# Moving some products of two state space loops from VectorE to GpSimd

## The chip, the cores and the metric

The kernel runs on one core of a Trainium2 chip, as one program for a whole network of four layers. A core has five engines with a queue of instructions each: TensorE (PE in the profile, with its weight loads as PEld), VectorE (DVE), ScalarE (ACT), GpSimd (POOL) and SyncE (SP), which here issues the DMAs. Each engine works its queue in order and waits on semaphores for the others.

The metric is the device time of one execution in microseconds. Before the change the median of 3 runs was 2389.74 us (2386.41 to 2395.51).

## The reference

The network is a chain of residual blocks on x of shape (4, 512, 128). Two of the blocks, `L2_attn_b` and `L3_attn_b`, are selective state space layers of the same form. Cut to what matters, one of them is

```python
xz = x @ in_proj                                # 256 inner channels and 256 gates
u = silu(causal_conv4(xi) + conv_b)             # xi, z = the halves of xz
dtr, Bc, Cc = split(u @ x_proj)                 # 64, 16 and 16 columns
delta = softplus(dtr @ dt_proj + dt_bias)
A = -exp(A_log)                                 # 256 channels x 16 states
def step(h, inp):
    d_t, b_t, c_t, u_t = inp
    dA = exp(d_t[:, :, None] * A)               # the decay
    h = dA * h + (d_t * u_t)[:, :, None] * b_t[:, None, :]
    return h, einsum('bdn,bn->bd', h, c_t)
y = scan(step) over 512 tokens
out = ((y + u * D) * silu(z)) @ out_proj
```

Four batches, 256 channels, 16 states and 512 tokens make 4 x 256 x 16 = 16384 independent recurrences of 512 steps in each of the two layers.

## The kernel before

The function `mamba` runs once for `L2b` and once for `L3b`. A *unit* n is 256 recurrences: two halves t, each of 8 channels by 16 states on the 128 partitions, with 512 tokens along the free dimension, so a unit's tiles are 128 x 2 x 512. There are 16 units per batch and 64 units per loop, n = 0 to 63. One unit passes these steps:

- `fetch(n)` (L2424): two DMAs on SP bring delta of the unit's channels, repeated over the states, from DRAM into a ring of six SBUF buffers `da`.
- `decay(n)` (L2439): two ScalarE activations, exp(A * delta), in place in `da`. The first column of the second half holds 0, set once, which restarts the recurrence there; the activation and the DMA leave it out.
- `gain(n)` (matmuls through the helper at L346): TensorE spreads delta*u from the channels over the 128 rows, into a PSUM tile `ps_du` of two banks, three buffers.
- `product(n)` (L2453): VectorE multiplies `ps_du` by B, in place in PSUM.
- `scan(n)` (L2458): VectorE's scan computes h = a*h + x over 1024 columns, a from `da`, x from `ps_du`, the result into an SBUF tile `hc` with seven buffers. Then GpSimd multiplies `hc` by C in place (L2463); VectorE does this for the last unit alone (L2461).
- `read(n)`: for a pair of units, eight matmuls sum over the states into `ps_y`.

The main loop (L2515) sets the order by hand. In iteration n it traces fetch(n+5), product(n+1), scan(n), gain(n+2), decay(n+3), then the *pieces* whose time has come, and in odd iterations read(n-5) for units n-5 and n-4. Compute instructions are pinned behind what was traced before them on their engine (`keep`, `pin=True`), so this is also the order in each of the four queues.

The pieces prepare the next batch beside the current one (`prepare`, L2280): the convolution in four parts (c0a, c0b, c1a, c1b) with a ScalarE activation `raw` after each second part; u (Silu); xd, a projection copied to SBUF by ScalarE (L2325); dt0 and dt1, each a matmul and two activations that read its bank, `dl` and `e` (L2291); br and cr (projections of B and C); exps and logs (softplus); z0, z1 and sz (the gate); and s00 to s13, eight sums on GpSimd (L2356) with two stores of delta to DRAM (L2360). Counted from the first unit of the batch prepared, the usual times are

```python
order = (
    "c0a", "c0b", "c1a", "c1b", "u", "xd", "dt0", "dt1", "br", "exps", "logs", "s00",
    "s01", "z0", "s02", "s10", "z1", "s11", "cr", "s12", "s03", "sz", "s13",
)
usual = (
    -6, -5, -4, -3, -2, -1, 0, 1, 2, 3, 4, 5,
    6, 6, 7, 8, 8, 9, 9, 10, 11, 11, 12,
)
```

Batches 2 and 3 use these; so dt0 of batch 2 is in iteration 16 and that of batch 3 in iteration 32. Batch 1 is prepared from iteration 0 on by its own list. While batch 3 runs, nothing is left to prepare.

PSUM has eight banks: six for `ps_du`, one for `ps_y`, and a single one, tag "mm", that all the matmuls of the pieces share. When consecutive ScalarE functions are in different tables, a table load (ACT_TABLE_LOAD) stands before the second: Silu or Ln in the pieces, Exp in the decays. Copies in the trace are not preceded by one.

Of the kernel before, what the change touches and what calls it, by code (L numbers as in the profile page):

```python
# [11 lines left out]
F32 = mybir.dt.float32  # L12
AF = mybir.ActivationFunctionType
ALU = mybir.AluOpType
# [4 lines left out]
P = 128  # L19
B, S, D = 4, 512, 128  # L20
# [254 lines left out]
class Net:  # L275
# [1977 lines left out]
    def mamba(self, g):  # L2253
# [5 lines left out]
        nc, tc = self.nc, self.tc  # L2259
        LAG, SPREAD, AHEAD, FETCH = 4, 2, 3, 5  # L2260
        with ExitStack() as es:
            sp = es.enter_context(tc.tile_pool(name=g + "_s", bufs=1))
            rp = es.enter_context(tc.tile_pool(name=g + "_r", bufs=2))
            pp = es.enter_context(tc.tile_pool(name=g + "_p", bufs=1, space=PSUM))
            dp = es.enter_context(tc.tile_pool(name=g + "_d", bufs=2, space=DRAM))
            keep = tc.keep_in_program_order
            m0 = self.m
            w, am, wc, dram = m0["w"], m0["am"], m0["wc"], m0["dram"]
# [6 lines left out]
            def bank(name):  # L2275
                return pp.tile([P, S], F32, tag="mm", name=name)
# [3 lines left out]
            def prepare(b, **when):  # L2280

                u, sz, dl, du, br, cr = sets[b % 2]
                xb = b * S
                t = {}
# [29 lines left out]
                def project(out, at, n):  # L2314
                    ps = bank("ps_d")
                    for c in range(2):
                        self.mm(
                            ps[:n],
                            w["xp"][:, c * 320 + at : c * 320 + at + n],
                            u[:, c],  # L2320
                            start=c == 0,
                            stop=c == 1,
                            pin=True,
                        )
                    keep(nc.scalar.copy(out, ps[:n]))  # L2325

                def xd():
                    t["xd"] = rp.tile([64, S], F32, name="xd", bufs=1)
                    project(t["xd"], 0, 64)

                def step(c):
# [30 lines left out]
                for name, n in when.items():  # L2362
                    f = {
                        "c0a": (conv, 0, False),
                        "c0b": (conv, 0, True),
                        "c1a": (conv, 1, False),
                        "c1b": (conv, 1, True),
                        "u": (lambda: act(u, t["raw"], AF.Silu),),
                        "xd": (xd,),
                        "dt0": (step, 0),  # L2370
                        "dt1": (step, 1),
                        "br": (project, br, 64, P),
                        "cr": (project, cr, 192, P),
                        "exps": (exps,),
                        "logs": (logs,),
                        "z0": (gate, 0),
                        "z1": (gate, 1),
                        "sz": (lambda: act(sz, t["z"], AF.Silu),),
                        **{f"s{c}{k}": (sums, c, k) for c in range(2) for k in range(4)},
                    }[name]  # L2380
                    pieces.append((n, f))
# [10 lines left out]
            for b in range(2, B):  # L2392
                at = {p: 16 * (b - 1) + n for p, n in zip(order, usual)}
# [13 lines left out]
            dx, hc, yp, y, po = {}, {}, {}, {}, {}  # L2407
# [3 lines left out]
            da = {n: ring[n % 6] for n in range(16 * B)}  # L2411

            def place(n):
                b, k = divmod(n, 16)
                c, k = divmod(k, 8)
                i, h = divmod(k, 2)
                return b, c, i, h

            def fetch(n):

                b, c, i, h = place(n)
                for t in range(2):
                    m = 4 * (2 * t + h) + i
                    nc.sync.dma_start(  # L2424
                        da[n][:, t, t:],
                        dram[b][8 * m : 8 * m + 8, c, t:].unsqueeze(0).to_broadcast([16, 8, S - t]),
                    )

            def decay(n):
                b, c, i, h = place(n)  # L2430
                for t in range(2):
                    at = 16 * c + 4 * (2 * t + h) + i
                    src = da[n][:, t]
                    if n < SPREAD:
                        r = slice(64 * t, 64 * t + 64)
                        src = pp.tile([P, S], F32, tag="y", name="ps_dl") if t else bank("ps_dl")
                        self.mm(src, spread[r, 4 * h + i], sets[0][2][r, c], pin=True)
                    keep(
                        nc.scalar.activation(  # L2439
                            da[n][:, t, t:], src[:, t:], AF.Exp, scale=am[:, at : at + 1]  # L2440
                        )
                    )

            def gain(n):
                b, c, i, h = place(n)
                dx[n] = pp.tile([P, 2, S], F32, tag="du", name="ps_du", bufs=3)
                for t in range(2):
                    r = slice(64 * t, 64 * t + 64)
                    self.mm(dx[n][:, t], spread[r, 4 * h + i], sets[b % 2][3][r, c], pin=True)

            def product(n):
                br = sets[n // 16 % 2][4].unsqueeze(1).to_broadcast([P, 2, S])
                keep(nc.vector.tensor_tensor(dx[n], dx[n], br, ALU.mult))  # L2453

            def scan(n):
                hc[n] = rp.tile([P, 2, S], F32, name="hc", bufs=7)
                h, a, x = (t.rearrange("p t s -> p (t s)") for t in (hc[n], da[n], dx[n]))
                keep(nc.vector.tensor_tensor_scan(h, a, x, 0.0, ALU.mult, ALU.add))  # L2458
                cr = sets[n // 16 % 2][5].unsqueeze(1).to_broadcast([P, 2, S])
                if n == 16 * B - 1:  # L2460
                    keep(nc.vector.tensor_tensor(hc[n], hc[n], cr, ALU.mult))  # L2461
                else:
                    keep(nc.gpsimd.tensor_tensor(hc[n], hc[n], cr, ALU.mult))  # L2463

            def read(n):

                b, c, i, _ = place(n)
                if n % 8 == 0:
                    yp[c] = pp.tile([P, S], F32, tag="y", name="ps_y")
                    self.mm(yp[c], skip[:, c], sets[b % 2][0][:, c], stop=False, pin=True)  # L2470
                    if c == 0:
                        y[b] = rp.tile([P, 2, S], F32, name="y", bufs=1)
                for h in range(2):
                    for t in range(2):
                        r = 32 * (2 * t + h)
                        self.mm(
                            yp[c][r : r + 32],
                            gather[:, i],
                            hc[n + h][:, t],
                            start=False,  # L2480
                            stop=i == 3,
                            pin=True,
                        )
# [18 lines left out]
            if g == "L2b":  # L2502
                self.roots(B - 1, B, keep)
            self.prime(AF.Exp)
            decay(0)
            gain(0)
            gain(1)
            product(0)
            if g == "L2b":
                self.centred(B - 1, keep)  # L2510
            decay(1)
            for n in range(SPREAD, FETCH):
                fetch(n)
            decay(2)
            for n in range(16 * B + 10):  # L2515
                if n + FETCH < 16 * B:
                    fetch(n + FETCH)
                if n + 1 < 16 * B:
                    product(n + 1)
                if n < 16 * B:  # L2520
                    scan(n)
                if n + 2 < 16 * B:
                    gain(n + 2)
                if n + AHEAD < 16 * B:
                    decay(n + AHEAD)
                while pieces and pieces[0][0] < n + 1:
                    f, *a = pieces.pop(0)[1]
                    f(*a)
                m = n - 1 - LAG
                if n % 2 == 1 and 0 <= m < 16 * B:  # L2530
                    read(m)
                    if m % 8 == 6:
                        last = m == 16 * B - 2
                        plan.at(n if last else n + 1, gated, m // 16, m // 8 % 2)
                        if m % 16 == 14:
                            plan.at(n if last else n + 4, output, m // 16)
                            plan.at(
                                n if last else n + 5,
                                lambda b: self.add_to_x(b, po[b], keep),
                                m // 16,  # L2540
                            )
                plan.run(n)
# [472 lines left out]
```

## Time and profile before

| | |
|---|---|
| median of 3 runs | 2389.74 us |
| profiled execution: its own time | 2384.57 us |
| profiled execution: span | 2382.5 us |
| mean granted TensorE clock | 0.944 |
| PE busy | 2131.7 us (89%) |
| VectorE busy | 1700.4 us (71%) |
| ScalarE busy | 1267.4 us (53%) |
| GpSimd busy | 630.7 us (26%) |
| first loop, unit 0's scan to unit 63's | 1570.79 to 1798.2 us |
| second loop, unit 0's scan to unit 63's | 2103.00 to 2335.8 us |

The two loops are about a fifth of the span. The shares above are over the whole program; what bounds the loops is read from windows inside them.

How to read the profile's lines. A group line gives the line of the code, the engine, the operation, out<-in by the program's names, the shapes and the count; then busy us in all and the mean ns of one; then the idle time of that engine just before these instructions and what ended most of it ("<-PE ps_du L346": a matmul that wrote ps_du). A window line gives the stretch, its length, then the busy us of PE, PEld, DVE, ACT and POOL with counts, then the granted clock, the share of the DMA engines and GB/s. A timeline line gives start, duration, engine, line, operation and count, with the idle time before it in brackets.

### The profile page before, as it was taken

To read this page: it belongs to the slowest core of one execution; us is meant where nothing else is said; L and a number is where in the kernel's file an instruction comes from. 1 tells how busy PE (TensorE), PEld (TensorE's weight loads), DVE (VectorE), ACT (ScalarE), POOL (GpSimd) and SP (SyncE) were. 2 spreads that over 40 slices of the span, in tenths; PEclk is the share of its full clock that TensorE was granted. 3 is DMA by queue.
4 is the path that set the end of the run, shared out by engine and by line. 5 is a ranking of instruction groups with operands and counts; after the bars stand their busy time and mean duration, and the time that the engine had idled before them with its cause. 6 is when DMAs were issued, how large, how long until landed. Compare 5 with 4: busy or idle time off the path is not lost. (4 is left out here: it accounts for less than half of the span.)

```text
span 2382.5 us, 33560 instructions
## 1 busy us (share of the span) xinstructions
PE 2131.7 (89%) x12196; PEld 1012.4 (42%) x12196; DVE 1700.4 (71%) x3219; ACT 1267.4 (53%) x2531; POOL 630.7 (26%) x474
## 2 busy tenths in 40 slices
PE   7999999999899998999877789988869998878868
PEld 2343334643233334568545446542214666422213
DVE  6666666579999774756455664678997657688995
ACT  4555554159855665343343453666644445476643
POOL 1001000010000001021354510048872015148871
PEclk9999999999799998999879989999989999998989
DMA  3000000600000000600200015344552520044550
GB/s 146 1 1 1 1 1 15 130 1 2 1 2 3 1 1 1 133 11 2 109 1 1 0 39 96 71 124 146 156 149 46 113 38 2 1 133 141 155 154 18
DMA packets 68884, 127.84 MB, mean 54 GB/s; under 512 B 9328, under 2 KB 29296, under 8 KB 68080
## 3 DMA queue, kind: packets, MB, share of 16 engines
q1 hardware_dynamic: 68720, 125.71, 20.4%
q8 instruction: 96, 1.57, 0.3%
q14 instruction: 68, 0.56, 0.1%
HBM read 119.91 MB, written 5.64 MB: 53 GB/s over the span
## 5 line engine op out<-in xcount | busy, mean ns | idle before, releaser
L2463 POOL TENSOR_TENSOR hc<-hc,cr 128x1024 f32<-128x1024 f32 x126 | 297.5, 2362 | 113.6 <-DVE hc L2458 107.9
L2458 DVE TENSOR_TENSOR_SCAN hc<-da,ps_du 128x1024 f32<-128x1024 f32 x128 | 291.0, 2275 | 0.0
L346 PE MATMUL ps_s<-k,q 32*128 32x512 f32 (+3 forms) x1088 | 247.8, 597 | 13.4 <-DVE mx L853 4.8
L540 ACT ACTIVATE e<-ps_s,mx 128x512 f32<-128x512 f32 x256 | 172.6, 686 | 139.4 <-DVE mx L535 132.8
L346 PE MATMUL ps_du<-du,spread 64*128 64x512 f32 x512 | 161.7, 704 | 64.2 <-DVE hc L2458 63.9
L2439 ACT ACTIVATE da<-da,am 128x512 f32<-128x512 f32 x248 | 165.7, 715 | 62.1 <-DMA da<-dram 48.4
L346 PE MATMUL ps<-xT,w_L2f 128*128 128x512 f32 (+1 forms) x416 | 190.6, 605 | 0.2 <-DVE t L2030 0.2
L939 DVE TENSOR_REDUCE nm<-ps_s 128x1 f32<-128x512 f32 x256 | 162.4, 683 | 36.6 <-PE ps_s L346 26.4
L1025 ACT ACTIVATE e<-ps_st 128x512 f32<-128x512 f32 x256 | 138.3, 595 | 89.2 <-PE ps_s L346 61.5
L535 DVE TENSOR_REDUCE mx<-ps_s 128x2 f32<-128x1024 f32 x128 | 150.9, 1219 | 43.8 <-PE ps_s L346 43.6
L2453 DVE TENSOR_TENSOR ps_du<-ps_du,br 128x1024 f32<-128x1024 f32 x128 | 154.9, 1211 | 26.5 <-PE ps_du L346 26.4
L864 ACT ACTIVATE e<-e,mx 128x512 f32<-128x512 f32 (+3 forms) x256 | 140.1, 548 | 17.2 <-DVE mx L853 16.9
L346 PE MATMUL ps_st<-q,k 32*128 32x512 f32 x512 | 143.8, 646 | 0.0
L346 PE MATMUL ps_s<-q,k 64*128 64x512 f32 x512 | 129.1, 618 | 2.2 <-ACT e L540 1.7
L346 PE MATMUL ps_c<-e,vz 128*64 128x512 f32 x512 | 123.5, 604 | 0.8 <-POOL vz L551 0.8
L661 DVE TENSOR_TENSOR hc<-hc,wt 128x1024 f32<-128x1024 f32 x80 | 93.6, 1170 | 37.8 <-DMA wt<-dram 19.5
L2030 DVE SCALAR_TENSOR_TENSOR t<-ps,w_L2f,t 128x512 f32<-128x512 f32 (+1 forms) x104 | 76.9, 746 | 60.9 <-PE ps L346 37.3
L551 POOL TENSOR_TENSOR vz<-v,z 128x512 f32<-128x512 f32 x32 | 33.4, 1043 | 321.9 <-DVE z L549 292.9
L346 PEld LDWEIGHTS ps_du<-du,spread 64*128 64x128 f32 x512 | 45.4, 201 | 171.7 <-issue 126.4
L853 DVE CUSTOM_DVE_ANT_0 e<-ps_s,tri 128x512 f32<-128x512 f32 (+3 forms) x256 | 109.2, 484 | 12.3 <-PE ps_s L346 12.1
L346 PEld LDWEIGHTS ps_s<-k,q 32*128 32x128 f32 x1088 | 85.8, 192 | 75.5 <-issue 35.0
L346 PEld LDWEIGHTS ps<-xT,w_L2f 128*128 128x128 f32 (+1 forms) x416 | 74.7, 188 | 96.5 <-issue 79.0
(505 smaller groups left out, 4149.9 us busy)
## 6 DMA issues: line engine op xcount, KB each, us to landing
da<-dram SPq DMA_DIRECT2D x124, 256.0 KB
da<-dram SPq DMA_DIRECT2D x124, 255.5 KB
wt<-dram SPq DMA_DIRECT2D x144, 128.0 KB
wt<-dram SPq DMA_DIRECT2D x32, 256.0 KB
dram<-dl SPq DMA_DIRECT2D x16, 256.0 KB
wt<-dram SPq DMA_DIRECT2D x16, 224.0 KB
wt<-dram SPq DMA_DIRECT2D x16, 192.0 KB
wt<-dram SPq DMA_DIRECT2D x16, 160.0 KB
```

The costliest lines, as they stand in the source:

```text
L346: i = self.nc.tensor.matmul(out, lhsT, rhs, start=start, stop=stop)
L535: nc.vector.tensor_reduce(mx, sc, AX.X, ALU.max, negate=True)
L540: nc.scalar.activation(es[n][:, hh], sc[:, hh], AF.Exp, bias=mx[:, hh : hh + 1], accum_out=z[m][:, j, hh : hh + 1],)
L661: nc.vector.tensor_tensor(h, h, wt[b, k][:, r:e], ALU.mult)
L853: red = nc.vector.tensor_tensor_reduce(e[:, i, :w], sc[i][:, :w], tri[:, S - w :], -1.0, BIG, ALU.add, ALU.min, mx[:, i : i + 1],)
L864: nc.scalar.activation(e[:, i, :w], e[:, i, :w], AF.Exp, bias=mx[:, i : i + 1], scale=-1.0, accum_out=z[:, i : i + 1],)
L939: nc.vector.tensor_reduce(nm[:, j, i, 9:10], sc, AX.X, ALU.max, negate=True)
L1025: keep(nc.scalar.activation(es_[n][:, i], sc, AF.Exp))
L2439: nc.scalar.activation(da[n][:, t, t:], src[:, t:], AF.Exp, scale=am[:, at : at + 1])
L2453: keep(nc.vector.tensor_tensor(dx[n], dx[n], br, ALU.mult))
L2458: keep(nc.vector.tensor_tensor_scan(h, a, x, 0.0, ALU.mult, ALU.add))
L2463: keep(nc.gpsimd.tensor_tensor(hc[n], hc[n], cr, ALU.mult))
```

## The change

In each loop 11 of the 64 units, called *shared*, take another way: n = 2, 5, 15, 18, 31, 34, 47, 50, 53, 56 and 59. For a shared unit

- `product(n)` becomes a ScalarE copy of `ps_du` (128 x 1024) into the unit's `hc` tile and a GpSimd multiplication by B in place in `hc`;
- `decay(n)` writes its exponentials into the PSUM banks of `ps_du`, which the copy has read, and a third, small ScalarE copy brings the zero column along;
- `scan(n)` takes a from PSUM and x from `hc`, and writes `hc` in place.

In the order, gain and product of a shared unit n+2 are traced in iteration n before scan(n), and its decay after scan(n), in place of one iteration earlier. The decays of the other units stay three ahead. `hc` has eight buffers instead of seven, and the small tile xd lies in the `du` tile of the batch being prepared, which is written later.

```diff
                 def xd():
-                    t["xd"] = rp.tile([64, S], F32, name="xd", bufs=1)
+                    t["xd"] = du[:64, 0]
                     project(t["xd"], 0, 64)
...
                         self.mm(src, spread[r, 4 * h + i], sets[0][2][r, c], pin=True)
+                    out = dx[n] if n in shared else da[n]
                     keep(
                         nc.scalar.activation(
-                            da[n][:, t, t:], src[:, t:], AF.Exp, scale=am[:, at : at + 1]
+                            out[:, t, t:], src[:, t:], AF.Exp, scale=am[:, at : at + 1]
                         )
                     )
+                if n in shared:
+                    keep(nc.scalar.copy(dx[n][:, 1, 0:1], da[n][:, 1, 0:1]))
...
+            shared = (2, 5, 15, 18, 31, 34, 47, 50, 53, 56, 59)
+
             def product(n):
                 br = sets[n // 16 % 2][4].unsqueeze(1).to_broadcast([P, 2, S])
-                keep(nc.vector.tensor_tensor(dx[n], dx[n], br, ALU.mult))
+                if n in shared:
+                    hc[n] = rp.tile([P, 2, S], F32, name="hc", bufs=8)
+                    keep(nc.scalar.copy(hc[n], dx[n]))
+                    keep(nc.gpsimd.tensor_tensor(hc[n], hc[n], br, ALU.mult))
+                else:
+                    keep(nc.vector.tensor_tensor(dx[n], dx[n], br, ALU.mult))
 
             def scan(n):
-                hc[n] = rp.tile([P, 2, S], F32, name="hc", bufs=7)
-                h, a, x = (t.rearrange("p t s -> p (t s)") for t in (hc[n], da[n], dx[n]))
+                if n in shared:
+                    a, x = dx[n], hc[n]
+                else:
+                    hc[n] = rp.tile([P, 2, S], F32, name="hc", bufs=8)
+                    a, x = da[n], dx[n]
+                h, a, x = (t.rearrange("p t s -> p (t s)") for t in (hc[n], a, x))
                 keep(nc.vector.tensor_tensor_scan(h, a, x, 0.0, ALU.mult, ALU.add))
...
             for n in range(SPREAD, FETCH):
                 fetch(n)
-            decay(2)
             for n in range(16 * B + 10):
                 if n + FETCH < 16 * B:
                     fetch(n + FETCH)
-                if n + 1 < 16 * B:
+                if n + 1 < 16 * B and n + 1 not in shared:
                     product(n + 1)
+                if n + 2 in shared:
+                    gain(n + 2)
+                    product(n + 2)
                 if n < 16 * B:
                     scan(n)
-                if n + 2 < 16 * B:
+                if n + 2 in shared:
+                    decay(n + 2)
+                elif n + 2 < 16 * B:
                     gain(n + 2)
-                if n + AHEAD < 16 * B:
+                if n + AHEAD < 16 * B and n + AHEAD not in shared:
                     decay(n + AHEAD)
```

## The prediction

> **What bounds the kernel now.** I read the page's busy shares and slices first, then its costliest groups, then the table of windows over the two state space loops, last the timeline inside them. VectorE is called DVE, ScalarE ACT, GpSimd POOL and TensorE PE. These are the loop's groups (busy us, mean ns | idle before, releaser):
>
> ```profile
> L2463 POOL TENSOR_TENSOR hc<-hc,cr 128x1024 f32<-128x1024 f32 x126 | 297.5, 2362 | 113.6 <-DVE hc L2458 107.9
> L2458 DVE TENSOR_TENSOR_SCAN hc<-da,ps_du 128x1024 f32<-128x1024 f32 x128 | 291.0, 2275 | 0.0
> L2439 ACT ACTIVATE da<-da,am 128x512 f32<-128x512 f32 x248 | 165.7, 715 | 62.1 <-DMA da<-dram 48.4
> L2453 DVE TENSOR_TENSOR ps_du<-ps_du,br 128x1024 f32<-128x1024 f32 x128 | 154.9, 1211 | 26.5 <-PE ps_du L346 26.4
> ```
>
> The scans never idle, POOL mostly waits for them. The windows (busy us of PE, PEld, DVE, ACT, POOL) of the first loop say the same:
>
> ```profile
> 1620.00:1680.00 60.00, 53.09 (x194) 16.07 (x192) 59.04 (x47) 39.48 (x56) 50.73 (x27) 0.94 0.53 157
> 1680.00:1740.00 60.00, 50.02 (x186) 14.23 (x186) 59.41 (x46) 42.98 (x58) 50.34 (x27) 0.89 0.54 155
> 1740.00:1800.00 60.00, 39.25 (x164) 10.16 (x160) 59.83 (x45) 20.99 (x30) 40.70 (x18) 0.86 0.40 114
> ```
>
> DVE is busy 98 to 99.7% there. Scan starts on the timeline stand 3.31 us apart: 2.19 for the scan, 1.12 for the product between two scans (the last two scans, with no product between, take 4.45 us together). So a product is worth 1.12 us, less than its 1.21 us row, since neighbours overlap. By busy time PE has little to spare; ACT and POOL have most in the last window, where no next batch is prepared.
>
> The share does not say who waits for ACT. The timeline around units 16 to 20 does (rows of POOL, DMA and weight loads left out):
>
> ```profile
> 1623.33 1.98 PE L346 MATMUL ps_x<-xT,wc 128*128 128x510 f32 x4
> ...
> 1625.34 0.69 ACT L2291 ACTIVATE raw<-ps_x,w_L2b 128x512 f32<-128x512 f32 x1 [3.80 <-PE ps_x L346]
> ...
> 1630.58 1.28 ACT L2439 ACT_TABLE_LOAD   x1
> ...
> 1632.52 1.13 PE L346 MATMUL ps_du<-du,spread 64*128 64x512 f32 x4
> ...
> 1633.58 1.33 ACT L2439 ACTIVATE da<-da,am 128x512 f32<-128x512 f32 x2
> ...
> 1633.73 1.12 PE L346 MATMUL ps_dt<-xd,w_L2b 64*128 64x512 f32 x2
> 1634.89 0.69 ACT L2291 ACTIVATE dl<-ps_dt,w_L2b 128x512 f32<-128x512 f32 x1
> ...
> 1635.47 0.68 ACT L2291 ACTIVATE e<-ps_dt,w_L2b 128x512 f32<-128x512 f32 x1
> ...
> 1636.20 1.12 PE L346 MATMUL ps_dt<-xd,w_L2b 64*128 64x512 f32 x2
> ...
> 1637.26 1.06 PE L346 MATMUL ps_y<-hc,gather 128*32 128x512 f32 x8
> ...
> 1638.44 1.13 PE L346 MATMUL ps_du<-du,spread 64*128 64x512 f32 x4
> ...
> 1641.52 1.21 DVE L2453 TENSOR_TENSOR ps_du<-ps_du,br 128x1024 f32<-128x1024 f32 x1
> ```
>
> Counting scans from 1570.79 (unit 0), 1632.52 is gain(18), 1638.44 gain(20), 1641.52 product(20). All preparing matmuls share one PSUM bank ("mm"). The second dt matmul (1636.20) starts when ACT has read the first one's bank twice (last read ends 1636.15), and gain(20) stands behind it in PE's queue. So whatever ACT does in front of those two reads moves gain(20), which today is done 2.0 us before product(20) needs it (1639.57 to 1641.52).
>
> **The change part by part.** Each loop has 11 shared units, each sized by its place.
>
> *Removed:* 22 products, 22 x 1.12 = 24.6 us, if nothing else becomes late.
>
> *Added on POOL:* 22 x 2.36 us, the row of the C product, same shape and engine. POOL has 113.6 us of idle before its C products. The mean spare is enough; in the last batch units 50, 53, 56, 59 stand three apart: three units give DVE 3 x 3.31 - 1.12 = 8.8 us and POOL 4 x 2.33 = 9.3 (two in a row take 4.68). POOL falls back 0.5 us each time, part of which DVE's gating (0.6) and adding to x with its moments (2.3) give back. I take 0.9 us lost per loop, between 0 and 2.
>
> *Added on ACT:* a 128x1024 copy from PSUM. Rows: 0.58 for half of it from PSUM (xT copies, 0.583), 1.05 for 128x1024 from SBUF (1049); bounds 0.9 and 1.16 (two halves). I take 1.0 of queue time, near the 1.05 row less the 0.1 by which neighbours overlap. The exponentials into PSUM have no row; 0.68 (out of PSUM) and 0.72 (SBUF) are nearest: 0.61 each in the queue (a pair takes 1.33), within 0.06. The one-column copy: 0.1, from a 128x1 activation of 0.20. POOL's multiply waits for the copy; queued behind it is the C product of two units earlier, for which PE's reads wait four units later (13 us), so they don't notice.
>
> *Moved:* the shared unit's decays from one unit ahead in ACT's queue to behind its copy, thus behind its gain. Today they run while ACT waits (3.80 us idle before 1625.34). The next unit's decays, and the pieces of the iteration, queue behind them; the single bank makes PE wait for those pieces. This decides.
>
> Units 18 and 34 (iterations 16 and 32, where dt0 lies). After gain(18), done 1633.65, ACT has: copy 1.0, table load 1.28 (now paid at 1630.58, before decay(18)), two exponentials 1.22, column 0.1, decay(19) 1.22, then the two reads, 0.58 and 0.69. With 0.1 of hand-over that is 6.1 to 6.2: the second dt matmul starts near 1639.85 instead of 1636.20, 3.65 late. Behind it come the read (1.06 + 1.03 queue time) and gain(20) (1.13): done 1643.1, against 1641.52.
>
> Units 15 and 31. gain(15) at 1622.27 ends 1623.40; copy 1.0, own decays 1.22, column 0.1, decay(16) 1.22 put the raw activation at 1627.05 instead of 1625.34, 1.7 late. That shifts u, xd and gain(18) by 1.7, as the table load, u, xd follow each other without slack. Pair 15 and 18: product(20) at 1643.1 + 1.7 = 1644.8, so **+3.3** net, both products already taken out. The rows at 1680 to 1698 repeat these (raw 1682.29, dt 1693.16, product(36) 1698.47): again **+3.3**.
>
> Unit 5. gain(5) ends at 1582.69. Copy, two decays, column and decay(6) (3.55 with hand-over) push the Silu table load from 1583.60 to 1586.3 and u with it: xd on PE, already idle 1.68 us waiting for u, goes 2.7 later, gain(7) and dt0 behind it. Product(8) waits for PE today (0.33 us), so it passes the whole **+2.7** on. The second loop's rows (raw 2114.72, load 2116.65) give the same.
>
> Unit 2: product(3) comes at 1576.41, when gain(3) comes from behind PE's convolutions: the saving becomes a wait, **0**.
>
> Units 47, 50, 53, 56, 59: no pieces, ACT idle two thirds: 5 x -1.12 = -5.6, with POOL's 0.9, **-4.7**.
>
> *Costed at nothing:* xd in du: its last older reader, a gain two units before on the same engine, is done; without that cover its copy would wait one gain, 1.13. The eighth hc buffer covers taking a buffer two units early; without it the copy would wait for a read, 1.06. SP's fetches stay as many; a shared unit's delta buffer comes free earlier, after its decays.
>
> **Sum.** Per loop 0 + 2.7 + 3.3 + 3.3 - 4.7 = +4.6; two loops **+9.2 us**. Against the profiled execution (span 2382.5, 2.1 around it, 2384.57) that is 2393.8; that execution lies 5.2 under the median of 2389.74, which becomes **2399**. The copy's bounds move it by -1 to +1.6 (five copies per loop on the late chain), the exponentials' by 1.2 either way, POOL's by -1.8 to +2.2.
>
> **A rule against the change.** POOL's row is 2.36 against 1.21 on DVE, and 1.35 for a product with C on DVE. The Trainium skill, GPSIMD Engine Reference, section 4.1 (Engine selection), says elementwise work belongs on VectorE, about twice as fast for two inputs. By that rule alone, had every moved product lain on the path, 22 x (2.36 - 1.12) = +27 us, 2417. The idle row says POOL's time is mostly hidden, so I don't take it; I get a loss from ACT's order, which that rule does not speak of.
>
> **The rivals.**
>
> *It does what it says (faster).* The late chain counts only if the second dt matmul starts later than 1637.2: product(20) would stand at 1640.4, and 3.2 us follow the matmul. ACT has 1.0 us of room there and I count 3.65. If the block fitted (ACT's work shorter, or overlapping gain's wait), ten units per loop would keep 1.12: 2 x (-11.2 + 0.9) = -20.6, 2369; half of the stalls left gives about 2384. For it: ACT's mean share of 66 to 72%. Against: each queue keeps the code's order, and the waits read above are already PE's.
>
> *PE is slow in the new waits (slower).* gain took 1.9 to 2.1 instead of 1.13 at 1734.74, 1748.58 and 1784.56, and the granted clock is 0.86 to 0.89 in the later windows against 0.94. A slow gain or read in a late chain adds about 0.9. Four per loop add 7.2: 2406; seven per loop 12.6: 2412. It decides from +2.8 above my sum on, where 0.5% is passed: three slow groups in all. Against: at 1632 to 1643 all ran at 1.13.
>
> **How the numbers follow.** A change of 0.5%, 12 us, is about what a measurement of this kernel can tell from none: 2377.8 to 2401.7. My sum, with the unknown rows, 0.57: +4 to +15, 0.42 of it within 0.5% and 0.15 slower. Slow PE, 0.27: +12 to +25, slower. As intended, 0.16: -24 to -5, 0.12 faster and 0.04 within. Together faster 0.12, same 0.46, slower 0.42. My own case spans 2394 to 2405; for eight in ten I take 2376 to 2413, which leaves out most of the full saving and the worst of slow PE.
>
> **What would show it.** Right: product rows 106 on DVE, 22 multiplies with br at about 2.36 on POOL; DVE's idle before products grown from 26.5 us to 55 or so (net loss plus products taken out, 3.8 + 5.5 + 5.5 + 1.1 per loop, a little of it before scans), new ones at products 7, 20 and 36; the second dt matmul waiting for ACT 6 us after gain(18) and gain(34); the last batch about 4.7 us shorter. Wrong: scans 2.19 apart at 18 and 34 and no new ps_du wait (then the first rival), DVE waiting for hc from POOL more than 2 us per loop, or a copy or exponential beyond my bounds.

## The result and the profile after

| | before | after |
|---|---|---|
| median of 4 runs each | 2388.07 us | 2417.24 us (2415.41 to 2418.80) |
| profiled execution: its own time | 2384.57 us | 2415.41 us |
| profiled execution: span | 2382.5 us | 2413.4 us |
| mean granted TensorE clock | 0.944 | 0.939 |
| first loop, unit 0's scan to unit 63's | 227.4 us | 242.4 us |
| second loop, unit 0's scan to unit 63's | 232.8 us | 246.6 us |

The change makes the kernel slower by 29 us: ratio 1.0125, 95% interval 1.0106 to 1.0144. That is 4 us above the upper end of the forecast range and 18 above the forecast itself. Of the 30.9 us that the span grew, 28.9 lie inside the two loops (15.1 and 13.9).

The costliest groups of the page after (busy us, mean ns | idle before, releaser) answer to those shown in the prediction:

```profile
L2477 POOL TENSOR_TENSOR hc<-hc,cr 128x1024 f32<-128x1024 f32 x126 | 295.1, 2357 | 66.1 <-DVE hc L2472 60.7
L2472 DVE TENSOR_TENSOR_SCAN hc<-da,ps_du 128x1024 f32<-128x1024 f32 x106 | 239.0, 2273 | 1.2 <-PE ps_y L346 1.2
L2463 DVE TENSOR_TENSOR ps_du<-ps_du,br 128x1024 f32<-128x1024 f32 x106 | 128.8, 1216 | 69.9 <-PE ps_du L346 69.7
L2440 ACT ACTIVATE da<-da,am 128x512 f32<-128x512 f32 x204 | 133.2, 712 | 2.5 <-DMA da<-dram 1.6
```

VectorE lost 22 products (128 to 106 rows) and gained 43.4 us of idle time in front of the others (26.5 to 69.9), 69.7 us of it waiting for a gain on TensorE. The new instructions, from the groups by engine, have rows of the size that the prediction expected:

```profile
L2460 ACT COPY hc<-ps_du 128x1024 f32<-128x1024 f32 x22 | 22.3, 1013 | 70.9 <-PE ps_du L346 70.9
L2440 ACT ACTIVATE ps_du<-da,am 128x512 f32<-128x512 f32 x22 | 15.2, 692 | 0.6
L2445 ACT COPY ps_du<-da 128x1 f32<-128x1 f32 x22 | 3.6, 163 | 0.8
L2461 POOL TENSOR_TENSOR hc<-hc,br 128x1024 f32<-128x1024 f32 x22 | 51.9, 2360 | 26.6 <-ACT hc L2460 26.6
L2472 DVE TENSOR_TENSOR_SCAN hc<-ps_du,hc 128x1024 f32<-128x1024 f32 x22 | 50.2, 2283 | 4.8 <-ACT ps_du L2445 4.6 <-POOL hc L2461 0.2
```

The windows of the first loop (length, then busy us of PE, PEld, DVE, ACT, POOL, granted clock, DMA share, GB/s) show where it went. VectorE was busy 98 to 99.7% before in each third; now 85 and 84% in the first two, where batches are prepared, and 98% in the last.

```profile
1620.00:1680.00 60.00, 46.97 (x182) 14.51 (x180) 51.03 (x40) 39.12 (x56) 47.61 (x25) 0.94 0.50 140
1680.00:1740.00 60.00, 48.38 (x170) 14.60 (x168) 50.55 (x40) 37.59 (x54) 49.01 (x25) 0.89 0.47 140
1740.00:1812.00 72.00, 52.04 (x210) 13.93 (x210) 70.82 (x51) 37.17 (x56) 67.08 (x32) 0.83 0.47 135
```

The timeline around unit 18 has the forecast chain, in its forecast order (rows of GpSimd, DMA and weight loads left out):

```profile
1639.76 1.13 PE L346 MATMUL ps_du<-du,spread 64*128 64x512 f32 x4
...
1640.98 1.01 ACT L2460 COPY hc<-ps_du 128x1024 f32<-128x1024 f32 x1 [1.54 <-PE ps_du L346]
...
1642.02 1.28 ACT L2440 ACT_TABLE_LOAD   x1
...
1643.31 1.42 ACT L2440 ACTIVATE ps_du<-da,am 128x512 f32<-128x512 f32 x2
...
1644.76 0.16 ACT L2445 COPY ps_du<-da 128x1 f32<-128x1 f32 x1
1644.86 1.33 ACT L2440 ACTIVATE da<-da,am 128x512 f32<-128x512 f32 x2
...
1646.09 0.67 ACT L2291 ACTIVATE dl<-ps_dt,w_L2b 128x512 f32<-128x512 f32 x1
1646.66 0.67 ACT L2291 ACTIVATE e<-ps_dt,w_L2b 128x512 f32<-128x512 f32 x1
...
1647.39 2.07 PE L346 MATMUL ps_dt<-du,w_L2b 64*128 64x512 f32 x2 [4.79 <-ACT e L2291]
...
1649.39 1.93 PE L346 MATMUL ps_y<-hc,gather 128*32 128x512 f32 x8
...
1651.25 1.54 PE L346 MATMUL ps_du<-du,spread 64*128 64x512 f32 x4
...
1652.84 1.23 DVE L2463 TENSOR_TENSOR ps_du<-ps_du,br 128x1024 f32<-128x1024 f32 x1 [5.53 <-PE ps_du L346]
```

From the end of gain(18), 1640.89, to the second dt matmul it is 6.50 us; the prediction counted 6.1 to 6.2. New is what comes behind: dt matmul, read and gain take 2.07, 1.93 and 1.54 us. In the same places before they took 1.12, 1.06 and 1.13. The windows of the profile after around this place and around unit 5's late u say why; the eighth column, ahead of the DMA share, is the granted clock of TensorE:

```profile
1584.00:1588.30 4.30, 0.00 (x0) 0.00 (x0) 3.73 (x3) 4.17 (x7) 4.30 (x3) 0.88 0.82 229
1588.30:1594.00 5.70, 5.69 (x9) 1.80 (x10) 0.00 (x0) 4.41 (x6) 3.97 (x2) 0.50 0.26 87
...
1637.00:1642.00 5.00, 5.00 (x21) 1.68 (x22) 5.00 (x3) 2.38 (x3) 3.00 (x2) 1.00 0.17 20
1642.00:1647.40 5.40, 0.61 (x3) 0.01 (x1) 3.96 (x3) 5.31 (x9) 5.33 (x3) 0.81 0.91 256
1647.40:1653.00 5.60, 5.60 (x15) 1.47 (x16) 0.16 (x1) 3.64 (x6) 3.95 (x2) 0.58 0.11 28
```

TensorE idles for almost 5 us, since ScalarE is late, and then does the overdue work at 0.50 to 0.58 of its clock, while VectorE stands (0.00 and 0.16 us busy). Before, the clock read 1.00 at the first of these places through the whole stretch of 1576 to 1600. There the projection xd and the gain behind u are, before and then after:

```profile
1586.00 1.93 PE L346 MATMUL ps_d<-u,w_L2b 128*64 128x512 f32 x4 [1.68 <-ACT u L2291]
...
1587.86 1.13 PE L346 MATMUL ps_du<-du,spread 64*128 64x512 f32 x4
```

```profile
1588.31 3.67 PE L346 MATMUL ps_d<-u,w_L2b 128*64 128x512 f32 x4 [4.89 <-ACT u L2291]
...
1591.92 2.08 PE L346 MATMUL ps_du<-du,spread 64*128 64x512 f32 x4
```

The Trainium skill, TensorE: Matmul & The Clock Gate, Part 1, states such a rule: a stretch of some 3.4 us without work halves the clock, and about as long a busy stretch brings it back. The two long waits here agree with it; shorter waits, here and in the experiments below, do not keep to the figure.

### The profile page after: what moved, and what is told of

Same layout as the page of the kernel before. It is cut to its first block, busy times and chain, and to the rows that moved or that the text cites. A ratio compares the mean times of both kernels' runs of the same rounds, so it can differ in the third digit from the quotient of the medians.

```text
span 2413.4 us, 33534 instructions
## 1 busy us (share of the span) xinstructions
PE 2140.5 (89%) x12196; PEld 1016.1 (42%) x12196; DVE 1678.6 (70%) x3197; ACT 1290.4 (53%) x2575; POOL 679.0 (28%) x496
## 5 line engine op out<-in xcount | busy, mean ns | idle before, releaser
L2472 DVE TENSOR_TENSOR_SCAN hc<-da,ps_du 128x1024 f32<-128x1024 f32 x106 | 239.0, 2273 | 1.2 <-PE ps_y L346 1.2
L2463 DVE TENSOR_TENSOR ps_du<-ps_du,br 128x1024 f32<-128x1024 f32 x106 | 128.8, 1216 | 69.9 <-PE ps_du L346 69.7
L2440 ACT ACTIVATE da<-da,am 128x512 f32<-128x512 f32 x204 | 133.2, 712 | 2.5 <-DMA da<-dram 1.6
```

The lines of the kernel that those rows point to most:

```text
L2440: nc.scalar.activation(out[:, t, t:], src[:, t:], AF.Exp, scale=am[:, at : at + 1])
```

## The experiments

Theories: **A (place and clock).** The way itself saves 1.1 us a unit. The loss is that a shared unit's copy and exponentials stand on ScalarE ahead of a read that TensorE waits for (the late chain), and that TensorE then runs at half clock. **B (the way costs).** Copy, GpSimd product and scan from PSUM cost more than they save wherever they stand. **C (queue only).** The late chains alone, with longer ScalarE work than counted; the clock is a bystander.

All in one table; the loops' change is from unit 0's scan to unit 63's in the profiled execution, against before (227.4 and 232.8).

| kernel | shared units a loop | median us (before) | ratio, 95% interval | loop 1 | loop 2 |
|---|---|---|---|---|---|
| the change | 11 | 2417.24 (2388.07) | 1.0125 [1.0106, 1.0144] | +15.1 | +13.9 |
| e1_late5 | 5 | 2379.06 (2385.72) | 0.9971 [0.9959, 0.9982] | -2.9 | -3.3 |
| e2_moved | 11 | 2390.50 (2385.72) | 1.0022 [1.0011, 1.0033] | +0.5 | +3.7 |
| e3_warm | 11 | 2414.33 (2385.72) | 1.0131 [1.0115, 1.0148] | +11.5 | +14.3 |
| e4_decays_in_sbuf | 11 | 2404.99 (2385.72) | 1.0092 [1.0077, 1.0107] | +9.7 | +11.4 |
| e5_best | 8 | 2370.39 (2386.68) | 0.9929 [0.9914, 0.9944] | -8.7 | -6.3 |
| e6_no5 | 10 | 2405.12 (2386.68) | 1.0080 [1.0061, 1.0100] | +8.5 | +14.0 |
| e7_order | 11 | 2406.90 (2386.68) | 1.0085 [1.0066, 1.0104] | +8.3 | +10.6 |
| e8_warm2 | 11 | 2402.99 (2386.68) | 1.0067 [1.0050, 1.0084] | +8.9 | +7.4 |
| e9_more | 13 | 2377.81 (2386.42) | 0.9955 [0.9940, 0.9971] | -4.4 | -1.7 |
| e10_order_and_warm | 11 | 2395.67 (2386.42) | 1.0037 [1.0024, 1.0051] | +1.8 | +7.3 |
| e11_without_8 | 12 | 2367.61 (2385.78) | 0.9919 [0.9906, 0.9933] | -9.0 | -7.5 |
| e12_nine | 9 | 2364.51 (2385.78) | 0.9913 [0.9897, 0.9930] | -10.1 | -7.4 |

The runs came in batches with their own runs of before, so kernels of different batches are compared by their ratios; 0.001 is 2.4 us.

### The last batch alone

```diff
-            shared = (2, 5, 15, 18, 31, 34, 47, 50, 53, 56, 59)
+            shared = (47, 50, 53, 56, 59)
...
+            decay(2)
             for n in range(16 * B + 10):
```

> Only the five shared units of the last batch (47, 50, 53, 56, 59) stay in each loop; the six others take the old way. Theory A (the loss comes from the shared units that lie beside the preparation of the next batch, where ScalarE's moved work holds TensorE): the last batch of the changed kernel already shows the gain, 4.2 us in the first loop and 5.0 in the second, so this kernel is about 9 us faster than before (2379, between 2375 and 2383). Rival B (the other way of a shared unit costs more in itself, by GpSimd's slower product or by the traffic to PSUM): 29 us over 22 units is 1.3 us each, so 10 units cost +13 us against before (2401).

It is faster than before, by 0.3%. The same five units that the change has in its last batch save 3.6 us there in the first loop and 4.2 in the second (scan of unit 63 against that of unit 45). The way itself saves; B falls, unless something about it is worse in the other batches.

### Units 18 and 34 moved two on

```diff
-            shared = (2, 5, 15, 18, 31, 34, 47, 50, 53, 56, 59)
+            shared = (2, 5, 15, 20, 31, 36, 47, 50, 53, 56, 59)
```

> As the changed kernel, with units 18 and 34 exchanged for 20 and 36: the same number of copies, products and decays, but no longer in the iterations of the first dt piece (16 and 32). Theory A: the scans of units 16 to 20 and 32 to 36 lost 6.6, 6.5, 7.0 and 5.4 us in the changed kernel (25.5 together); ScalarE's extra block no longer stands before the two reads of the dt bank, so these go, and units 20 and 36 save 1.1 each: about 2387 to 2392, against 2417. Rival B: nothing of the count has changed, so 2417 as it is.

The count of new instructions is the same, and the ratio is 0.0103 lower, 25 us. Two units a loop, each two places off, carry most of the loss: with 20 and 36 the copy is behind dt0's reads instead of ahead. Unit 5 stays dear (scan 6 late by 4.9 in the first loop).

### A few more matmuls against the clock

```diff
                 b, c, i, h = place(n)
-                dx[n] = pp.tile([P, 2, S], F32, tag="du", name="ps_du", bufs=3)
+                if n not in dx:
+                    dx[n] = pp.tile([P, 2, S], F32, tag="du", name="ps_du", bufs=3)
...
                 elif n + 2 < 16 * B:
-                    gain(n + 2)
+                    for _ in range(4 if n + 2 in (19, 35) else 1):
+                        gain(n + 2)
```

> As the changed kernel, but the gain of units 19 and 35 is computed four times over (same values), so that TensorE works on for some 3.2 us in the place where it now stands idle for 4.8 before the second dt matmul. If the clock is what made the loss larger than forecast (after that wait the granted clock was 0.58 and dt, read and gain took 2.07, 1.93 and 1.54 instead of 1.12, 1.06 and 1.13): products 20 and 36 come some 2.2 us earlier, four places, 8 to 9 us less than the changed kernel (2408). If the wait itself is all that counts and the clock is a bystander: the same 2417, or a little more by product 19 being 3 us later.

The ratio did not move by more than its interval, and by itself this spoke for C. The timeline of this kernel at unit 18 shows that the edit had not kept the clock up:

```profile
1648.32 1.12 PE L346 MATMUL ps_dt<-du,w_L2b 64*128 64x512 f32 x2 [2.22 <-ACT e L2291]
1649.37 1.75 PE L346 MATMUL ps_y<-hc,gather 128*32 128x512 f32 x8
...
1651.05 2.08 PE L346 MATMUL ps_du<-du,spread 64*128 64x512 f32 x4
```

With the wait cut from 4.79 to 2.22 us the dt matmul ran in full 1.12, and then the clock fell all the same, under the read and the gain that the scans wait for. The run told nothing between A and C; e8_warm2 repeats it with the waits filled.

### The decays left in SBUF

```diff
-                    out = dx[n] if n in shared else da[n]
+                    out = da[n]
...
-                if n in shared:
-                    keep(nc.scalar.copy(dx[n][:, 1, 0:1], da[n][:, 1, 0:1]))
...
-                    a, x = dx[n], hc[n]
+                    a, x = da[n], hc[n]
...
+            decay(2)
...
-                if n + 2 in shared:
-                    decay(n + 2)
-                elif n + 2 < 16 * B:
+                if n + 2 not in shared and n + 2 < 16 * B:
                     gain(n + 2)
-                if n + AHEAD < 16 * B and n + AHEAD not in shared:
+                if n + AHEAD < 16 * B:
                     decay(n + AHEAD)
```

> The other half of the change undone: the 11 units' products stay on GpSimd behind ScalarE's copy, but their decays stay in place in SBUF and three units ahead, as before; no column copy; their scans read both inputs from SBUF. Theory A: in front of the dt reads ScalarE now has copy 1.0 and one unit's decays 1.2 after the gain, so the second dt matmul is 1.05 us late where there was 1.0 of room; raw is 0.4 late, u of batch 1 about 1.0 late. So the pairs 15+18 and 31+34 save some 1.8 each, unit 5 nothing, the last batch 4.7: some 8 us per loop, 2372 (2366 to 2382). Rival B: copy and product are still there, so most of the loss stays, 2405 to 2417. A third way: a scan with two SBUF inputs may run slower beside GpSimd, or slow it; then the rows of those 22 scans or of the GpSimd products grow beyond 2.28 and 2.36 us.

The decays are off the late chain, and VectorE's idle time before products falls to 34.7 us, as A says. But most of the gain is eaten by something no part of the prediction had, and which the expectation named as its third way: with both inputs in SBUF the 22 scans take 3.78 us in the mean instead of 2.28, up to 4.44, and GpSimd's products with C beside them up to 4.37 instead of 2.36. The groups of this kernel:

```profile
L2470 DVE TENSOR_TENSOR_SCAN hc<-da,hc 128x1024 f32<-128x1024 f32 x22 | 83.2, 3782 | 1.9 <-POOL hc L2459 1.9
L2475 POOL TENSOR_TENSOR hc<-hc,cr 128x1024 f32<-128x1024 f32 x126 | 336.5, 2688 | 27.4 <-DVE hc L2470 21.7 <-PE ps_y L346 5.7
```

The Trainium skill, GPSIMD Engine Reference, section 8 (Key points), names it: the two engines share SBUF interfaces, and VectorE instructions with two SBUF inputs contend with GpSimd. The trace agrees: one of the 22 scans, at 2139.81 us, has no GpSimd instruction beside it, and it took 2.28 us. The scan at 1643.08 began 0.08 us behind the start of a product of 2.36 us and took 4.42. So the decays' place in PSUM, which put them behind the copy, is also what keeps these scans at 2.28.

### Eight units away from every late chain

```diff
-            shared = (2, 5, 15, 18, 31, 34, 47, 50, 53, 56, 59)
+            shared = (20, 36, 42, 50, 53, 56, 58, 61)
...
+            decay(2)
             for n in range(16 * B + 10):
```

> Eight units (20, 36, 42, 50, 53, 56, 58, 61) in the new way, none of them beside a read of dt0 or of u that the scans wait for. Placement theory: each shared unit saves VectorE one product, 1.12 us, less some 0.1 of waits; two loops make 16 units, so about 16 below before: 2370 (2366 to 2376), VectorE's products 112. Rival, the way itself costs: each shared unit is worth nothing or loses some 1.3 us as in the change as a whole (29 us over 22 units): 2386 to 2410.

2370.39, as A said; in the first loop eight units save 8.7 us, 1.08 each. VectorE's idle time before its 112 products is 27.6 us, about that of before with 128:

```profile
L2463 DVE TENSOR_TENSOR ps_du<-ps_du,br 128x1024 f32<-128x1024 f32 x112 | 135.7, 1212 | 27.6 <-PE ps_du L346 27.3
```

### The change without unit 5

```diff
-            shared = (2, 5, 15, 18, 31, 34, 47, 50, 53, 56, 59)
+            shared = (2, 15, 18, 31, 34, 47, 50, 53, 56, 59)
```

> The change without unit 5: ten units in the new way. The scans of the changed kernel fell behind by 6.4 us in the first loop and 7.3 in the second between units 4 and 8. If unit 5 alone makes that: 13.7 below the changed kernel, about 2403. By the prediction's own price for unit 5 (2.7 a loop): 2412. If something else before unit 8 makes it: 2417.

2405.12; 0.0045 in ratio, 11 us, between the prices of 6.4 and 7.3 a loop and the forecast's 2.7, nearer the former. In the first loop it is plain: scan 10 stands 0.1 us late instead of 5.6. In the second loop of the profiled execution nothing is won; there deltas landed late (ScalarE waited three times for the DMA of `da`, 0.32 to 0.58 us each), the second half of the convolution started 11.52 us into the loop instead of 10.19, and TensorE's clock was 0.66 between 2120 and 2130 us. That execution's own time is 2411.27, the highest of the four.

### The next unit's exponentials ahead of the copy

```diff
+                if n + 2 in shared and n + AHEAD < 16 * B:
+                    decay(n + AHEAD)
                 if n + 2 in shared:
                     gain(n + 2)
                     product(n + 2)
...
-                if n + AHEAD < 16 * B and n + AHEAD not in shared:
+                if n + AHEAD < 16 * B and not {n + 2, n + AHEAD} & set(shared):
```

> Same units, same work; on ScalarE the exps of the unit after a shared one stand ahead of the shared unit's copy instead of behind it and its exps. Chain theory: what stands behind the copy is late by the copy's 1.0 and its wait, so the raw exps of unit 15's pair and of unit 31's come some 1.3 earlier, the second dt matmul some 1.5 earlier, and with a shorter wait part of the clock loss goes (up to 2.2 in each of four places): 2397 to 2410. If the order on ScalarE does not matter: 2417.

The order on ScalarE alone, with the same work, is worth 0.0040, 9.5 us. The queue is a cause. In the first loop the steps at unit 5, at 15 and 18, and at 31 and 34 shrink from 5.6, 6.6 and 7.0 us to 3.6, 3.8 and 4.0; in the second the first ten units gain nothing (8.5 late instead of 7.0) and the pairs shrink to 2.1 and 3.3. The clock is not cured by it: the second dt matmul now waits 3.13 us instead of 4.79 and is still slow, with what follows it, in the timeline of this kernel:

```profile
1641.62 2.07 PE L346 MATMUL ps_dt<-du,w_L2b 64*128 64x512 f32 x2 [3.13 <-ACT e L2291]
1643.62 1.94 PE L346 MATMUL ps_y<-hc,gather 128*32 128x512 f32 x8
...
1645.49 2.08 PE L346 MATMUL ps_du<-du,spread 64*128 64x512 f32 x4
```

### TensorE kept busy in the waits

```diff
                 if n + 2 in shared:
                     decay(n + 2)
                 elif n + 2 < 16 * B:
-                    gain(n + 2)
+                    for _ in range(
+                        6 if n + 2 in (19, 35) or (n + 2 == 6 and g == "L2b") else 1
+                    ):
+                        gain(n + 2)
...
-            self.mm(ps, w["in"][:, 256 + c * P : 256 + c * P + P], xT[:, :S], pin=True)
+            for _ in range(7 if c == 0 and not spare else 1):
+                self.mm(ps, w["in"][:, 256 + c * P : 256 + c * P + P], xT[:, :S], pin=True)
```

> The change with matmuls repeated so that TensorE idles less ahead of the late second dt matmul (gains of 19 and 35 six times) and ahead of u (gain of 6 in the first loop six times, the first gate matmul of the second loop seven times). All repeats write what the first wrote. If the granted clock of 0.5 to 0.6 after the wait is what made these waits larger than forecast: product 7 of loop 1 about 2.1 us earlier, 6 of loop 2 about 1.9, 20 and 36 about 1.3 each in both loops, so some 9 below the changed kernel, 2408. If the clock is a bystander, or the repeats themselves get in the way: 2417 or more.

With the first change of e3_warm, so that a repeated gain writes the same tile. It only adds work to TensorE, and the time falls by 0.0058, 14 us. The windows over the two waits and what follows them, and the timeline at unit 18, in this kernel:

```profile
1584.30:1587.70 3.40, 2.82 (x14) 0.97 (x10) 0.53 (x1) 3.35 (x5) 3.40 (x3) 1.00 0.94 240
1587.70:1593.40 5.70, 5.55 (x16) 1.52 (x20) 5.53 (x4) 5.69 (x9) 4.06 (x2) 1.00 0.29 78
1642.00:1645.80 3.80, 3.31 (x14) 1.36 (x11) 0.44 (x1) 3.74 (x8) 3.80 (x3) 1.00 0.81 247
1645.80:1651.40 5.60, 5.59 (x22) 1.73 (x22) 5.35 (x4) 4.06 (x7) 4.04 (x2) 1.00 0.02 6
```

```profile
1645.81 1.12 PE L346 MATMUL ps_dt<-du,w_L2b 64*128 64x512 f32 x2 [0.50 <-ACT e L2292]
...
1646.86 1.07 PE L346 MATMUL ps_y<-hc,gather 128*32 128x512 f32 x8
...
1647.85 1.13 PE L346 MATMUL ps_du<-du,spread 64*128 64x512 f32 x4
```

The clock stays at 1.00 in both places and everything behind these waits takes its old time, though the second dt matmul comes no earlier: 6.51 us behind gain(18)'s end, where it was 6.50. The loops' shifts fall from 15.1 and 13.9 to 8.9 and 7.4. C falls: the clock makes about half of the loss. It makes at least that, since one wait that was not filled, of 2.56 us for u in the first loop, now had slow matmuls behind it: xd, read and gain(18) took 2.34, 1.94 and 1.44 us (from 1633.73 on) instead of 1.93, 1.06 and 1.13.

### Both cures together

The edits of the last two kernels in one.

> The change with both the other order on ScalarE and the repeated matmuls. If the late reads of dt0 and the slow clock after them are two terms that add: 10 and 14 below the changed kernel together, about 2393. If the other order's gain was itself the shorter idle time of TensorE, so that both cure the same thing: no better than the repeats alone, 2400 to 2404.

Of the change's 0.0125 the other order takes 0.0040, the repeats 0.0058, both together 0.0088 (21 us) of a sum of 0.0098. Within their intervals, queue and clock are two terms that add.

### More units, and which of them lose

```diff
-            shared = (20, 36, 42, 50, 53, 56, 58, 61)
+            shared = (8, 12, 20, 24, 28, 36, 40, 44, 50, 53, 56, 58, 61)
```

> Thirteen units a loop in the new way, one in four in the middle of a batch (8, 12, 20, 24, 28, 36, 40, 44) and 50, 53, 56, 58, 61; still none beside a read of dt0 or of u that the scans wait for. Placement theory: each is worth up to 1.1, so the five more in each loop are worth up to 11 more than the kernel with eight: 2360, at least 2365 if one in three is eaten by a later wait as unit 42's was. Rival: from here GpSimd sets the pace (four C products and one B product, 11.8 us, against four units of 12.1 on VectorE), its C products come late and the reads with them: 2370 or more.

2377.81: a little worse than with eight (0.9955 against 0.9929), and the number fits the rival. The place of the loss does not: 5.3 and 6.0 us go between units 7 and 10, in front of the later ones. The timeline there (the expectation had called unit 8 safe) shows the known chain again, with dt1 in the place of dt0, and a slow matmul behind it:

```profile
1595.65 1.01 ACT L2460 COPY hc<-ps_du 128x1024 f32<-128x1024 f32 x1 [1.85 <-PE ps_du L346]
...
1600.10 0.67 ACT L2291 ACTIVATE e<-ps_dt,w_L2b 128x512 f32<-128x512 f32 x1
...
1600.82 3.35 PE L346 MATMUL ps_d<-u,w_L2b 128*128 128x512 f32 x4 [3.51 <-ACT e L2291]
...
1606.55 1.23 DVE L2463 TENSOR_TENSOR ps_du<-ps_du,br 128x1024 f32<-128x1024 f32 x1 [5.13 <-PE ps_du L346]
```

So the next run took out unit 8 alone,

```diff
-            shared = (8, 12, 20, 24, 28, 36, 40, 44, 50, 53, 56, 58, 61)
+            shared = (12, 20, 24, 28, 36, 40, 44, 50, 53, 56, 58, 61)
```

> The kernel with thirteen units a loop, without unit 8. There the scans fell behind by 5.3 and 6.0 us between units 7 and 10, where ScalarE's queue held unit 8's copy and exps ahead of two reads of dt1, and TensorE waited 3.51 us for the second of them and then took 3.35 instead of 1.98 us. If that late read and the slow clock behind it are the cause: about 10 less than with unit 8, 2367 (2364 to 2370). If GpSimd's pace is the limit: 2376 to 2378.

which gives 0.0036 back (8.6 us). So the late read of dt1 and the clock behind it made this step, not GpSimd's pace. The groups of this kernel:

```profile
L2472 DVE TENSOR_TENSOR_SCAN hc<-da,ps_du 128x1024 f32<-128x1024 f32 x104 | 234.6, 2273 | 10.4 <-PE ps_y L346 10.4
L2463 DVE TENSOR_TENSOR ps_du<-ps_du,br 128x1024 f32<-128x1024 f32 x104 | 126.0, 1213 | 16.6 <-PE ps_du L346 16.5
L2472 DVE TENSOR_TENSOR_SCAN hc<-ps_du,hc 128x1024 f32<-128x1024 f32 x24 | 54.8, 2283 | 4.2 <-POOL hc L2461 4.2
```

VectorE waits 31.2 us in these three rows together, where it was 26.5 before. The scans' 10.4 us are an old wait in another row: 5.38 and 5.00 us lie ahead of one scan of each loop (1606.35 and 2136.50), where before a product waits 6.80 and 7.98 (1613.54 and 2151.62). The 4.2 us for GpSimd are new.

The last run took out three units whose saving the scans of the kernel with twelve soon lose again (12, 28 and 44):

```diff
-            shared = (12, 20, 24, 28, 36, 40, 44, 50, 53, 56, 58, 61)
+            shared = (20, 24, 36, 40, 50, 53, 56, 58, 61)
```

> Nine units a loop: 20, 24, 36, 40, 50, 53, 56, 58, 61, those that gained on VectorE in the kernel with thirteen without being taken back by a wait within two units. Placement theory: at or a little below the kernel with eight units: 2366 to 2371. If it is the number of units that matters (GpSimd's load), a step back toward the thirteen: 2372 to 2376.

Nine units save 10.1 us in the first loop, 1.12 each, the very price of the prediction. In the second loop 7.4: there 4.3 us went at unit 24 in the profiled execution. TensorE's clock was 0.68 between 2173 and 2180 us, the unit's copy waited 2.41 us for its gain, and VectorE then waited 3.08 us for a matmul (`ps_o`) that stood behind a ScalarE copy queued after the unit's exponentials. So unit 24 had a late chain in this loop, and lost only 0.4 us in the first. With 2364.51 it has the lowest median; its interval and those of the kernels with twelve and eight overlap, so the order among the three is open. All three beat before by 0.7 to 0.9%, and the change by 2%.

## Why the prediction was wrong

The direction of the likeliest case (a loss, from ScalarE's order) was right, its size was a third: +9.2 us in the span, where it was +30.9. Point by point, in scans of one unit against another, first loop and second:

| step | forecast | measured | with TensorE kept busy (e8_warm2) |
|---|---|---|---|
| units 2 and 5 (scan 10) | +2.7 | +5.6, +7.0 | +3.2, +4.6 |
| 15 and 18 (scan 20 against 10) | +3.3 | +6.6, +6.5 | +5.8, +3.5 |
| 31 and 34 (scan 40 against 20) | +3.3 | +7.0, +5.3 | +2.6, +4.3 |
| 47 to 59 (scan 63 against 40) | -4.7 | -4.2, -5.0 | -2.8, -5.0 |
| sum of a loop | +4.6 | +15.1, +13.9 | +8.9, +7.4 |

- **The saving per product and the last batch** were right: 1.12 forecast, 1.12 in e12_nine's first loop; -4.7 against -4.2 and -5.0. That the first loop of e12_nine meets 1.12 to the second digit is luck: e5_best's gives 1.08.
- **The new rows** were right within their bounds but for one: the copy 1.01, the product 2.36, the column copy 0.16 (0.10 in the queue). The two exponentials into PSUM take 1.45 us from the start of the first to that of the column copy, 0.72 each; forecast 0.61, within 0.06. They stand on every late chain. For the copy the groups of before have the very form, which the prediction overlooked: `em<-ps_s` (L2707), a copy of 128x1024 with a mean of 1013 ns; its 1.0 was right without that row. The scan from PSUM kept 2.28, which e4_decays_in_sbuf shows to be no matter of course.
- **The chain of unit 18** was right in all its links. From gain's end to the second dt matmul it is 6.50 us against 6.1 to 6.2, mostly by the exponentials. Product 20 came 6.0 us later against the scans before unit 15, where +3.3 was forecast; 2.2 of that difference are the three slow TensorE groups: (2.07 - 1.12) + (1.93 - 1.06) + (1.54 - 1.13).
- **The step that failed** is the sentence "Behind it come the read (1.06 + 1.03 queue time) and gain(20) (1.13)", and its like at units 5 and 34: the rows of a TensorE that had not waited were put behind a wait that the same paragraph had just made (3.65 us late by its count, a wait of 4.79 in the trace). They ran at about half the clock, and e8_warm2, where the wait is filled, shows that this costs 14 us. In the first loop unit 5 is the plainest: its load of the Silu table came 3.2 us later against the first scan (16.03 instead of 12.81) where 2.7 was forecast, and xd and the gain behind u then took 3.67 and 2.08 instead of 1.93 and 1.13, 2.7 more.
- **The second rival** had this mechanism, a slow gain or read at about 0.9 each, and was given 0.27. Its four in a loop (7.2 us) were too few: a late chain has not one slow group but two or three (2.2 to 2.8 us together, 1.2 at unit 5 of the second loop). Its seven (12.6 us) come near the 14 us, but the sum that they were added to was itself too low. Its evidence against (all ran at 1.13 at 1632 to 1643) was read at a place without the wait. The second loop of the same trace had evidence for it, where the prediction says that the rows give the same: behind a wait of 2.74 us (2119.54) the next gain took 2.05 us and xd 2.66.
- **What is left.** By the ratios the clock makes at least 0.0058, 14 us, of a miss of 21.7 in the span. The sums of the last column lie 4.3 and 2.8 over the forecast. Candidates are the longer exponentials, the slow matmuls ahead of gain(18) that e8_warm2 has in its first loop (1.6 us), its last batch in that loop, which saves 2.8 where 4.7 was forecast, and late deltas at the start of the second loop. The scans' wait for the column copy, 4.6 us in all over the 22 of the change, is gone in e8_warm2 and so is none of these. Which of the candidates makes how much stays open. The last 2 us lie outside the loops and are unexplained.
- **The first rival** (it does what it says) failed as a forecast for this list of units. For lists without late chains it holds: e5_best and e12_nine.
- **The rule on engine selection**, +27 us and 2417 by the rule alone, met the measured time by luck, not for its reason: it puts GpSimd's longer products on the path, while VectorE's wait for GpSimd is 0.2 us in the scans' row and 69.7 of the 69.9 us before products are TensorE's. With the same GpSimd products in other places the kernel is faster than before.

## What to carry to other kernels

Work moved to an engine with spare time is paid by whoever stands behind it in that engine's queue: go through the queue instruction by instruction up to the next read that a busy engine waits for, and put the work behind that read. If a step of a forecast makes TensorE wait some microseconds, cost what it does next at half its clock too, and look for all such instructions down to the one that the bottleneck needs. One list of eleven units lost 29 us and one of nine won 21 with the same code, so try the places before judging the way.

## What the runs showed of the hardware

- TensorE's clock fell to 0.50 and 0.58 behind waits of 4.9 and 4.8 us, and also behind shorter ones: 3.13 us in e7_order (2.07 for the dt matmul), and in e3_warm the first matmul behind a 2.22 us wait ran in full 1.12 and the next groups in 1.75 and 2.08. The figure of some 3.4 us that the Trainium skill gives (TensorE: Matmul & The Clock Gate, Part 1) is thus no safe lower bound in this kernel. The length of a wait alone did not decide: behind the waits of about 2.5 us for u ahead of dt0, xd took its full-rate 1.93 us at three places of the change and 2.59 at the fourth (1698.77), and before, a gain ran in 1.13 right behind 3.48 us (1781.25). Where the two long waits of e8_warm2's first loop were filled up to 0.5 and 0.6 us, the clock stayed at 1.00.
- Repeating matmuls that write the same values again, in waits that are there anyway, won 14 us (e8_warm2).
- A scan of 128 x 1024 with both inputs in SBUF takes up to 4.44 us beside GpSimd's multiplications instead of 2.28, and these up to 4.37 instead of 2.36; with one input in PSUM the means stay at 2.28 and 2.36. A single such scan with no GpSimd instruction beside it took 2.28. This contention cost most of what e4_decays_in_sbuf won on ScalarE.
